# Four-layer dense graph network on one core: first transfers in another order, narrower idle products, one chunk pair's features turned by VectorE, and a block of last-row work started later

## The chip, the cores and the metric

The kernel runs on one core of one Trainium2 chip. The metric is the time of one execution on the device in microseconds (us); the time shown before the change is the median of three runs. The profile is one further execution, recorded by the hardware profiler.

## The reference, cut to what matters

There are N = 3327 nodes with D = 64 features each, `x`, and one symmetric weighted adjacency matrix `adj` (3327 x 3327, about half a per cent of it other than zero). Four layers follow each other, each with a layer norm and a relu ahead and a residual behind. Every layer multiplies by the adjacency matrix or by a function of it, eight times in all.

```
def ggc(x, adj, W, wih, whh, bih, bhh):              # layer 0 has two of these cells
    gi = (adj @ (x @ W)) @ wih.T + bih
    gh = x @ whh.T + bhh
    r, z = sigmoid(gi_r + gh_r), sigmoid(gi_z + gh_z)
    n = tanh(gi_n + r * gh_n)
    return (1 - z) * n + z * x

h = relu(layernorm(x)); x = x + relu(ggc(relu(ggc(h, adj, ...1)), adj, ...2))   # k = 0, 1
h = relu(layernorm(x)); x = x + w(adj) @ (h @ weight) + bias                    # k = 2
#   w: mask of adj, each row's last 100 non-zeros weighted 0.5 ** (distance from the last)
h = relu(layernorm(x)); x = x + three times ((adj * adj) @ x) @ W.T + b         # k = 3, 4, 5
h = relu(layernorm(x)); x = x + two times tanh([adj @ x, x] @ W)                # k = 6, 7
```

## The kernel before, in words

**Tiles.** The nodes are padded to 3328 = 26 blocks of 128, kept as two halves `s` of 13 blocks. The 13 columns of blocks are cut into four chunks `c` of 3, 3, 3 and 4 blocks (`CH`); chunks 0 and 1 are group 0, chunks 2 and 3 are group 1. Features are kept in two forms: node-major tiles `y[k][c]` (128 nodes on the partitions, then block, half, feature), which are the stationary operands of the big products, and feature-major tiles `both[c]` (64 features of either half on the partitions, nodes along the row), on which the gates of a cell work.

**The big products.** For each of the eight steps `k`, each source block `q` and each chunk `c`, line 614 multiplies the 128 x 64 features of the block with the block's row of the transposed adjacency (384 or 512 columns for each of the two halves) into a PSUM bank `sum`. The row of a source block for one group is one tile `adj`, 768 KB for group 0 and 896 KB for group 1, read from memory by one DMA of SyncE's queue (line 412) into one of 20 slots. A tile is used for two steps where the order of sources allows it: `alone(0, 0)` runs step 0 of group 0, `joint(1, 0)` steps 0 and 1 of group 1, `joint(0, 1)` steps 1 and 2 of group 0, and so on, up to `alone(0, 7)`. Within `joint(1, 0)` step 1 takes its sources in the order: chunks 0 and 1, then chunk 2 (its half 0, then its half 1), then chunk 3 (the same).

**The order of the work.** Each engine works through its own instruction stream in order. The streams are written by one recorder, `run()`, which goes through the list of big products; after each of them it lets `spend` count down small tasks that were begun earlier and records their next part when their number of us has run out. These numbers are `yield`s: they are written by hand and decide where in the streams a piece of work stands, not when it runs. Slots, half slots for masks (`Mask`) and PSUM banks are handed out in the order of recording, and waits follow from reads and writes.

**The start.** SyncE's queue issues, in this order, the first three blocks of `x`, tile 0 of `adj`, the next blocks of `x` (`load_x(*CH[1])`), tiles 1 and 2, the last seven blocks of `x`, tile 3, the weights and the bias columns of the first cell (`load_cell`, lines 154 and 157), and from there on the tiles as slots come free. `warm_up` (line 177) issues 14 products of 384 columns whose result nobody reads. VectorE meanwhile makes the layer norm of chunk 0 and begins that of chunk 1 (lines 841 to 856; the power -0.5 on line 852 is GpSimd's).

**The counts.** Beside step 0, VectorE writes each tile as a 0/1 mask (line 473) into a half slot and TensorE sums it over source blocks (line 549), some tiles behind the product of the same tile.

**The cell.** When a chunk's sums of step 0 or 1 are complete, `gru` runs: `evacuate_stacked` copies half 0 of the sums to `both` on ScalarE (line 831) and half 1 on VectorE (line 832), TensorE makes three or four gate products from `both` (line 883), ScalarE the sigmoids (888) and the tanh (904), VectorE the rest (893 to 912), and ScalarE writes one of the two relus (915). After the first cell `after_0` turns the features back into the node-major form: `stacked_to_nodes` multiplies pieces of 64 nodes with an identity (line 781, 4 products of 64 columns for each block) and VectorE copies the result from PSUM (line 951). `transpose_on_vector` (line 810) and `sums_to_nodes` (line 826), used in later layers, turn features the other way, in squares of 32 by 32 on VectorE.

**The last rows.** The masks of step 2 give up row 127 to a row of counts, so that the 26 sources in row 127 are handled by themselves: `last_sources(g)` clears a half slot on GpSimd (line 571), loads the rows by two DMAs of SyncE's queue (575), makes one mask operation (577) and one combination with the counts (581) on VectorE and a conversion on ScalarE (583), over 768 or 896 columns. Its result is read at the end of step 2 of its group. It is begun with `later_task(130.0, ...)` for group 0 and `later_task(155.0, ...)` for group 1. In step 2 the products with `tri` (line 314) are evacuated to `e` alternately by ScalarE (530) and VectorE (528), three products ahead of their use on line 614.

Of the kernel before, what the change touches and what calls it, by code (L numbers as in the profile page):

```python
# [44 lines left out]
N, D = 3327, 64  # L45
P = 128
NB = 13
# [4 lines left out]
CH = [(0, 3), (3, 6), (6, 9), (9, 13), (3, 5), (5, 6)]  # L52
NC = 4
PARTS = (4, 5)
CWM = 512
GROUPS = [(0, 1), (2, 3)]
# [8 lines left out]
W1, IH1, HH1, W2, IH2, HH2 = 0, 1, 4, 7, 8, 11  # L65
# [26 lines left out]
def upper(n):  # L92
    return slice(n * D, (n + 1) * D)
# [3 lines left out]
def kernel(  # L97
# [9 lines left out]
    nc = tc.nc  # L107
# [7 lines left out]


    xs = const.tile([P, NB, 2, D], F32, name="xs")
    def load_x(g0, g1):
        nc.sync.dma_start(out=xs[:, g0:g1], in_=x[:, g0:g1])

    load_x(*CH[0])
    slots = [const.tile([P, 2, GWM], F32, name=f"adj{i}") for i in range(NBUF)]
    mhalf = const.tile([P, 8], F32, name="mhalf")
    nc.gpsimd.memset(mhalf, -0.5)
# [3 lines left out]
    stage = const.tile([P, 7 * D + NBIAS], F32, name="stage")  # L128
    w3 = const.tile([P, 2, 2, D], F32, name="w3")
    both = [const.tile([P, 2, (b1 - b0) * P], F32, name=f"both{c}") for c, (b0, b1) in enumerate(CH[:NC])]  # L130
# [4 lines left out]
    ident = const.tile([P, P], F32, name="ident")  # L135
# [15 lines left out]
                            compare_op=ALU.is_gt, fill=0.0, base=2 - P, channel_multiplier=1)  # L151

    def load_cell(cell):
        nc.sync.dma_start(out=stage[upper(0), :7 * D].rearrange("p (w f) -> p w f", f=D),
                          in_=weights[:, (W1, W2)[cell]:(W1, W2)[cell] + 7])
        if cell == 0:
            nc.sync.dma_start(out=stage[upper(0), 7 * D:], in_=bias_cols)

    def unfold_cell(cell):

# [11 lines left out]
    def warm_up():  # L172

        i, ps = take()
        for n in range(7):
            for h in range(2):
                nc.tensor.matmul(ps[upper(h), :width(0)], xs[:, 0, h, :], flat(xchunk(0)), start=True, stop=True)
        give(i)

    def fold_cell(cell):  # L180
# [67 lines left out]
    def more_constants():  # L248
# [32 lines left out]
        for c in range(NC):  # L281
            yield 4.0
            ahead_of_cell(c)
        yield 47.0
        load_cell(1)
        yield 20.0
        unfold_cell(1)
# [15 lines left out]
    def blocks(c):  # L303
        return CH[c][1] - CH[c][0]

    def width(c):
        return blocks(c) * P
# [15 lines left out]
    def take(sums=False, either=True):  # L323


        either = either and not sums
        pool = idle_sums if sums else idle_temps
        if either and idle_sums and (not pool or released[idle_sums[0]] < released[pool[0]]):
            pool = idle_sums
        for c in list(tasks):  # L330
            if not pool and c not in running:
                advance(c)
        i = pool.popleft()
        return i, banks[i]

    def give(i):
        released[i] = max(released) + 1
        (idle_sums if i < 4 else idle_temps).append(i)

    def nodes(c):  # L340

        return feat.tile([P, blocks(c), 2, D], F32, name=f"y{c}")

    def flat(t):
        return t.rearrange("p b s d -> p b (s d)")
# [4 lines left out]
    def xchunk(c):  # L350
        return xs[:, CH[c][0]:CH[c][1]]

    def view(ps, c):
        return ps[:, :width(c)].rearrange("p (b f) -> p b f", f=P)
# [5 lines left out]
    def advance(c):  # L360
        running.add(c)
        try:
            tasks[c][1] = next(tasks[c][0])
        except StopIteration:
            del tasks[c]
        running.discard(c)

    def begin(c, task):
        finish(c)
        tasks[c] = [task, 0.0]  # L370
        advance(c)

    def finish(c):
        while c in tasks:
            advance(c)

    def later_task(us, task):
        yield us
        yield from task
# [185 lines left out]
    def last_sources(g):  # L565

        w = sum(width(c) for c in GROUPS[g])
        w0 = CH[GROUPS[g][0]][0] * P
        room = Mask(w)
        v = room.view.rearrange("p s w -> p (s w)").bitcast(F32)  # L570
        nc.gpsimd.memset(v, 0.0)  # L571
        yield 4.0
        rows = adjT.rearrange("(q p) (s n) -> q p s n", p=P, s=2)
        for s in range(2):
            nc.sync.dma_start(out=v[s * D:s * D + NQ], in_=rows[:, P - 1, s, w0:w0 + w])
        yield 12.0
        nc.vector.tensor_scalar(v, v, 0.0, 129.0 * TWO7, op0=ALU.not_equal, op1=ALU.mult)
        for c in GROUPS[g]:
            finish(("count", c))
        yield 1.0  # L580
        nc.vector.scalar_tensor_tensor(v, totals[g], -TWO7, v, op0=ALU.mult, op1=ALU.add)
        yield 1.5
        nc.scalar.activation(lastw[g], v, AF.Relu, bias=bitsb)
        room.free()
# [37 lines left out]
    units = []  # L622
# [151 lines left out]
    def stacked_to_nodes(c, w):  # L774

        i, ps = take()
        v = view(ps, c)
        for b in range(blocks(c)):
            for s in range(2):
                for n in range(2):  # L780
                    nc.tensor.matmul(v[upper(n), b, upper(s)], both[c][:, s, b * P + n * D:b * P + (n + 1) * D], w(s),  # L781
                                     start=True, stop=True)
        return i, v
# [43 lines left out]
                yield 1.2  # L827
        return yk

    def evacuate_stacked(acc, c):  # L830
        nc.scalar.copy(both[c][upper(0), 0], acc[0][1][upper(0), :width(c)])  # L831
        nc.vector.tensor_copy(both[c][upper(1), 1], acc[1][1][upper(1), :width(c)])  # L832
        for i in {acc[0][0], acc[1][0]}:
            give(i)

# [36 lines left out]
    def gru(acc, c, bi, bh, cell, pace=1.0):  # L872

        w = width(c)
        evacuate_stacked(acc, c)
        yield 0.8 * pace
        at = dead.popleft()
        r, z, d = (slots[at].rearrange("p s w -> p (s w)")[:, i * CWM:i * CWM + w] for i in range(3))

        def gate(g):  # L880
            i, ps = take()
            for s in range(2):
                nc.tensor.matmul(ps[upper(1 - s), :w], cells[:, cell, s, g, :], both[c][:, s], start=True, stop=True)
            return i, ps

        for g, v in enumerate((r, z)):
            i, ps = gate(g)
            nc.scalar.activation(v, ps[:, :w], AF.Sigmoid, bias=bsum[:, cell, g:g + 1])
            give(i)
        nh = None if cell == 0 else gate(2)  # L890
        ni = gate(3)
        yield 1.0 * pace
        nc.vector.scalar_tensor_tensor(r, ahead[c] if nh is None else nh[1][:, :w], bcol[:, bh + 2:bh + 3], r,
                                       op0=ALU.add, op1=ALU.mult)
        nc.vector.tensor_tensor(r, r, ni[1][:, :w], ALU.add)
        give(ni[0])
        if nh is not None:
            give(nh[0])
        else:
            del ahead[c]  # L900
            if not any(ch in ahead for ch in GROUPS[c // 2]):
                rooms[c // 2].free()
        yield 1.0 * pace
        nc.scalar.activation(r, r, AF.Tanh, bias=bcol[:, bi + 2:bi + 3])
        yield 0.8 * pace
        for s in range(2):
            u = upper(1 - s)
            nc.vector.tensor_tensor(d[u], both[c][u, s], r[u], ALU.subtract)
        nc.vector.tensor_tensor(d, d, z, ALU.mult)
        nc.vector.tensor_tensor(d, d, r, ALU.add)  # L910
        if cell == 0:
            nc.vector.tensor_scalar(both[c][upper(0), 1], d[upper(0)], 0.0, None, op0=ALU.max)
        yield 2.4 * pace
        if cell == 0:
            nc.scalar.activation(both[c][upper(1), 0], d[upper(1)], AF.Relu)
            yield 1.0 * pace
        return at, d
# [27 lines left out]
    def after_0(c, acc):  # L945
        at, _ = yield from gru(acc, c, BI1, BH1, 0)
        dead.append(at)
        i, v = stacked_to_nodes(c, lambda s: ident[:, upper(1 - s)])
        yield 0.8
        yk = nodes(c)  # L950
        nc.vector.tensor_copy(flat(yk), v)
        give(i)
        y[1][c] = yk

    def after_1(c, acc):
# [62 lines left out]
    def after_7(c, acc):  # L1018
# [9 lines left out]
        nc.scalar.dma_start(out=out[:, g0:g1], in_=xs[:, g0:g1])  # L1028

    after[:] = [after_0, after_1, after_2, after_3, after_4, after_5, after_6, after_7]  # L1030


# [8 lines left out]
    alone(0, 7, sweep=6, parts=True)  # L1041

    nc.gpsimd.memset(stage, 0.0)
    first = list(dict.fromkeys(t for _, _, t in units))[:4]
    first[0].load()
    load_x(*CH[1])
    first[1].load()
    first[2].load()
    load_x(CH[2][0], NB)
    first[3].load()  # L1050
    load_cell(0)
    warm_up()
    for c in (0, 0, 0, 1, 0, 1, 1):
        if c in tasks:
# [4 lines left out]
    begin(2, later_task(4.0, before_0(2)))  # L1059
    begin(3, later_task(10.0, before_0(3)))  # L1060
    begin(NC + 1, later_task(130.0, last_sources(0)))
    begin(NC + 2, later_task(155.0, last_sources(1)))
    run()
    for c in list(tasks):
        finish(c)
# [39 lines left out]
```

## Time and profile before

| What | Value |
|---|---|
| median of 3 runs | 703.85 us (703.73 to 704.52) |
| the profiled execution | 704.14 us, of which the span of the program's own instructions is 702.2 us |
| TensorE, matrix products | 684.9 us busy, 98% of the span |
| VectorE | 348.8 us, 50% |
| ScalarE | 271.9 us, 39% |
| GpSimd | 80.5 us, 11% |
| bytes moved | 201.31 MB, 287 GB/s in the mean, 400 to 406 GB/s in each 10 us between 20 and 100 us |

The page gives the busy time of each engine over the span and in 40 slices of 17.6 us, the traffic, and the costliest groups of instructions, each with the idle time of its engine just before it and what ended most of that idle time. A matrix product of 32-bit numbers appears as two records, and its weight load is recorded apart (PEld). Records of products overlap, since the products are pipelined; the distance from one start to the next tells the pace. A busy share is a mean over stages that have different limits, so the stages are read one by one below.

### The profile page before, as it was taken

What the parts mean: (1) busy time and instruction counts of PE and PEld (TensorE: products, weight loads), DVE (VectorE), ACT (ScalarE), POOL (GpSimd) and SP (SyncE); (2) the same over time, 40 slices, a digit from 0 to 9 for tenths busy, and PEclk for the clock granted to TensorE, in tenths of its full rate; (3) what the DMA queues carried; (4) which work ended last, traced back from release to release, by engine and by line L of the source; (5) the groups of instructions that cost most, each with busy time, mean ns of one, the idle gap of its engine ahead of it and who ended that gap; (6) DMA issues with size and microseconds to landing.
All of it is one profiled execution on the core that took longest, in us unless ns stands there. A gap on an engine that the chain in (4) does not pass through costs nothing.

```text
span 702.2 us, 12670 instructions
## 1 busy us (share of the span) xinstructions
PE 684.9 (98%) x5128; PEld 378.0 (54%) x5128; DVE 348.8 (50%) x746; ACT 271.9 (39%) x422; POOL 80.5 (11%) x114
## 2 busy tenths in 40 slices
PE   7998999999999999999999999999999999999997
PEld 3684667744566686446444444333444444344586
DVE  4945835733997889747533106425271565005101
ACT  1112100212146878888998206832166600000101
POOL 5300000002284233011100000000000000000000
PEclk9999999999999999999999999999999999999999
DMA  8999998089776943683799659963998399917991
GB/s 312 401 402 404 406 406 278 1 295 401 252 240 257 385 162 101 235 290 100 268 386 347 237 179 408 405 250 122 385 366 270 107 398 405 406 73 273 403 403 49
DMA packets 68693, 201.31 MB, mean 287 GB/s; under 512 B 7244, under 2 KB 8372, under 8 KB 68636
## 3 DMA queue, kind: packets, MB, share of 16 engines
q1 hardware_dynamic: 65740, 199.46, 76.3%
q8 instruction: 40, 0.66, 0.4%
q10 hardware_dynamic: 720, 0.85, 0.3%
q0 software_dynamic: 2176, 0.20, 0.2%
q14 instruction: 17, 0.14, 0.1%
HBM read 199.45 MB, written 0.85 MB: 285 GB/s over the span
## 4 chain that ended last, share of the span: by engine, by line
PE 58%; DVE 1%; ACT 0%; POOL 0%; issue 0%; ACTq 0%; DVEq 0%; POOLq 0%
PE sum L614 54%; PE temp L314 3%; PE temp L781 1%; POOL st L852 0%; DVE xs L1026 0%; ACT t L1023 0%; DVE both L832 0%; ACT both L831 0%; DVE e L528 0%; ACTq L1028 0%; PE sum L314 0%; DVE y L848 0%; DVE t L843 0%; DVE y L856 0%; DVE st L849 0%
## 5 line engine op out<-in xcount | busy, mean ns | idle before, releaser
L614 PE MATMUL sum<-adj,y 128*64 128x384 f32 (+3 forms) x3016 | 535.8, 501 | 3.7 <-DMA adj<-in_adjT 2.5
L614 PEld LDWEIGHTS sum<-adj,y 128*64 128x64 f32 x3016 | 247.0, 137 | 233.8 <-issue 193.9
L447 ACT ACTIVATE adj<-adj 128x768 f32<-128x768 f32 (+1 forms) x176 | 144.2, 891 | 45.2 <-PE sum L614 22.8
L473 DVE TENSOR_SCALAR adj<-adj 128x768 bf16<-128x768 f32 (+3 forms) x208 | 113.5, 597 | 32.6 <-PE temp L549 24.7
L614 PE MATMUL sum<-e,both 128*64 128x384 bf16 (+1 forms) x624 | 73.9, 339 | 0.5 <-DVE e L528 0.5
L530 ACT ACTIVATE e<-temp,bitsb 128x384 int16<-128x384 f32 (+1 forms) x120 | 67.5, 608 | 14.4 <-PE temp L314 8.1
L831 ACT COPY both<-sum 64x384 f32<-64x384 f32 (+3 forms) x17 | 8.1, 478 | 151.2 <-PE sum L614 150.1
L832 DVE COPY both<-sum 64x384 f32<-64x384 f32 (+3 forms) x17 | 9.6, 568 | 109.7 <-ACT both L831 109.7
L852 POOL TENSOR_TENSOR st<-st,mhalf 128x6 f32<-128x6 f32 (+1 forms) x16 | 24.8, 1553 | 288.3 <-DVE st L850 288.3
L449 DVE TENSOR_TENSOR adj<-adj 128x768 f32<-128x768 f32 (+1 forms) x32 | 30.6, 1005 | 52.0 <-DMA adj<-in_adjT 33.3
L314 PE MATMUL temp<-adj,tri 128*64 128x384 bf16 (+1 forms) x332 | 51.4, 341 | 1.3 <-DVE e L528 1.2
L614 PEld LDWEIGHTS <-both 128*64 128x64 bf16 x624 | 41.2, 110 | 19.0 <-issue 6.5
L528 DVE TENSOR_SCALAR e<-temp 128x384 int16<-128x384 f32 (+1 forms) x46 | 28.3, 617 | 20.8 <-ACT e L530 10.9
L314 PEld LDWEIGHTS <-tri 128*64 128x64 bf16 x416 | 28.9, 110 | 17.4 <-issue 9.0
L478 POOL DMA_DIRECT2D adj<-totals x52 | 31.5, 607 | 51.6 <-PE temp L314 44.6
L810 DVE STREAM_TRANSPOSE both<-y 32x96 f32<-32x96 f32 (+1 forms) x128 | 35.6, 278 | 2.9
L549 PE MATMUL temp<-adj,behind 128*64 128x384 bf16 x208 | 33.7, 340 | 2.8 <-DVE adj L473 2.8
L826 DVE STREAM_TRANSPOSE y<-t 32x96 f32<-32x96 f32 (+1 forms) x64 | 17.8, 278 | 25.4 <-ACT t L817 24.5
L549 PEld LDWEIGHTS <-behind 128*64 128x64 bf16 x208 | 20.3, 110 | 16.6 <-issue 13.0
L762 DVE COPY t<-sum 128x384 f32<-128x384 f32 x6 | 3.3, 555 | 34.9 <-PE sum L614 34.9
L187 ACT COPY t<-temp 128x128 f32<-128x128 f32 x1 | 0.3, 266 | 48.2 <-PE temp L185 48.2
L571 POOL MEMSET adj<- 128x768 f32 (+1 forms) x2 | 1.9, 950 | 137.6 <-PE sum L614 137.6
(130 smaller groups left out, 353.3 us busy)
## 6 DMA issues: line engine op xcount, KB each, us to landing
adj<-in_adjT SPq DMA_DIRECT2D x130, 768.0 KB, 8.9
adj<-in_adjT SPq DMA_DIRECT2D x104, 896.0 KB, 12.1
xs<-in_x SPq DMA_DIRECT2D x1, 448.0 KB
adj<-totals POOLq DMA_DIRECT2D x26, 3.0 KB, 5.0
adj<-totals POOLq DMA_DIRECT2D x26, 3.5 KB, 3.2
xs<-in_x SPq DMA_DIRECT2D x2, 192.0 KB, 2.5
out<-xs ACTq DMA_DIRECT2D x2, 192.0 KB
out<-xs ACTq DMA_DIRECT2D x1, 256.0 KB
```

What stands on the lines that cost most here:

```text
L314: nc.tensor.matmul(out[hs], lhsT[:, hs], rhs, start=start, stop=stop)
L447: nc.scalar.activation(sq, v, AF.Square)
L449: nc.vector.tensor_tensor(sq, v, v, ALU.mult)
L473: nc.vector.tensor_scalar(t.mask.view[:rows, half], t.view()[:rows, half], 0.0, None, op0=ALU.not_equal)
L478: nc.gpsimd.dma_start(out=t.mask.view[P - 1:P], in_=totals[t.g][t.q:t.q + D + 1:D, :])
L528: nc.vector.tensor_scalar(wide[:, s], ps[:, :w], BITS, 0.0, op0=ALU.add, op1=ALU.max)
L530: nc.scalar.activation(wide[:, s], ps[:, :w], AF.Relu, bias=bitsb)
L549: nc.tensor.matmul(counts[c][1][s * D:(s + 1) * D, :w], behind[:, NQ - 1 - t.q:NQ - 1 - t.q + D], t.mask.view[:, s, t.cols(c)], start=firs ...
L614: nc.tensor.matmul(acc[h][1][h * D:(h + 1) * D, :w], yq[h], rhs[h], start=first and n == 0, stop=last and n == len(terms) - 1)
L810: nc.vector.transpose(to[at:at + 32, :, q], h[q * 32:(q + 1) * 32, :, s, f * 32:(f + 1) * 32])
L826: nc.vector.transpose(yk[q * 32:(q + 1) * 32, :, s, f * 32:(f + 1) * 32], v[at:at + 32, :, q])
L852: nc.gpsimd.tensor_tensor(st[:, 3, :n], st[:, 2, :n], mhalf[:, :n], ALU.pow)
```

## The change

The first blocks of `x` and the weights and bias columns of the first cell are issued from ScalarE's queue, except for the first three blocks of `x`, which stay on SyncE's; tile 0 of `adj` follows there at once. The idle products have 192 columns in place of 384. In the first cell `evacuate_stacked` makes both of its copies on ScalarE. `after_0` turns the features of chunks 2 and 3 by VectorE: for each half, eight operations of 32 partitions by 3 or 4 blocks of 32, in place of the products of line 781 and the copy of line 951. `last_sources(1)` is begun with 200 in place of 155; in the instruction streams its two VectorE operations then stand among the last operations of the stretch in which the second half of the layer norms of step 2, group 0, is made, its two DMAs stand 12 tile loads later in SyncE's queue, its memset behind four of the DMAs of the masks' last rows in GpSimd's, and its conversion behind the second tile of squares in ScalarE's. No other instruction of the four compute engines changes its place; some take another PSUM bank or slot.

```diff
--- before.py
+++ after.py
@@ -115,10 +115,8 @@
 
 
     xs = const.tile([P, NB, 2, D], F32, name="xs")
-    def load_x(g0, g1):
-        nc.sync.dma_start(out=xs[:, g0:g1], in_=x[:, g0:g1])
-
-    load_x(*CH[0])
+    for queue, (g0, g1) in ((nc.sync, CH[0]), (nc.scalar, CH[1]), (nc.scalar, (CH[2][0], NB))):
+        queue.dma_start(out=xs[:, g0:g1], in_=x[:, g0:g1])
     slots = [const.tile([P, 2, GWM], F32, name=f"adj{i}") for i in range(NBUF)]
     mhalf = const.tile([P, 8], F32, name="mhalf")
     nc.gpsimd.memset(mhalf, -0.5)
@@ -151,10 +149,11 @@
                             compare_op=ALU.is_gt, fill=0.0, base=2 - P, channel_multiplier=1)
 
     def load_cell(cell):
-        nc.sync.dma_start(out=stage[upper(0), :7 * D].rearrange("p (w f) -> p w f", f=D),
-                          in_=weights[:, (W1, W2)[cell]:(W1, W2)[cell] + 7])
+        queue = nc.sync if cell else nc.scalar
+        queue.dma_start(out=stage[upper(0), :7 * D].rearrange("p (w f) -> p w f", f=D),
+                        in_=weights[:, (W1, W2)[cell]:(W1, W2)[cell] + 7])
         if cell == 0:
-            nc.sync.dma_start(out=stage[upper(0), 7 * D:], in_=bias_cols)
+            queue.dma_start(out=stage[upper(0), 7 * D:], in_=bias_cols)
 
     def unfold_cell(cell):
 
@@ -174,7 +173,7 @@
         i, ps = take()
         for n in range(7):
             for h in range(2):
-                nc.tensor.matmul(ps[upper(h), :width(0)], xs[:, 0, h, :], flat(xchunk(0)), start=True, stop=True)
+                nc.tensor.matmul(ps[upper(h), :3 * D], xs[:, 0, h, :], xs[:, 0:3, 0], start=True, stop=True)
         give(i)
 
     def fold_cell(cell):
@@ -827,9 +826,12 @@
                 yield 1.2
         return yk
 
-    def evacuate_stacked(acc, c):
+    def evacuate_stacked(acc, c, on_scalar=False):
         nc.scalar.copy(both[c][upper(0), 0], acc[0][1][upper(0), :width(c)])
-        nc.vector.tensor_copy(both[c][upper(1), 1], acc[1][1][upper(1), :width(c)])
+        if on_scalar:
+            nc.scalar.copy(both[c][upper(1), 1], acc[1][1][upper(1), :width(c)])
+        else:
+            nc.vector.tensor_copy(both[c][upper(1), 1], acc[1][1][upper(1), :width(c)])
         for i in {acc[0][0], acc[1][0]}:
             give(i)
 
@@ -872,7 +874,7 @@
     def gru(acc, c, bi, bh, cell, pace=1.0):
 
         w = width(c)
-        evacuate_stacked(acc, c)
+        evacuate_stacked(acc, c, on_scalar=cell == 0)
         yield 0.8 * pace
         at = dead.popleft()
         r, z, d = (slots[at].rearrange("p s w -> p (s w)")[:, i * CWM:i * CWM + w] for i in range(3))
@@ -945,11 +947,20 @@
     def after_0(c, acc):
         at, _ = yield from gru(acc, c, BI1, BH1, 0)
         dead.append(at)
-        i, v = stacked_to_nodes(c, lambda s: ident[:, upper(1 - s)])
-        yield 0.8
         yk = nodes(c)
-        nc.vector.tensor_copy(flat(yk), v)
-        give(i)
+        if c in GROUPS[0]:
+            i, v = stacked_to_nodes(c, lambda s: ident[:, upper(1 - s)])
+            yield 0.8
+            nc.vector.tensor_copy(flat(yk), v)
+            give(i)
+        else:
+            for s in range(2):
+                v = both[c][upper(1 - s), s].rearrange("p (b q n) -> p b q n", q=4, n=32)
+                for f in range(2):
+                    for q in range(4):
+                        nc.vector.transpose(yk[q * 32:(q + 1) * 32, :, s, f * 32:(f + 1) * 32],
+                                            v[f * 32:(f + 1) * 32, :, q])
+                    yield 0.6
         y[1][c] = yk
 
     def after_1(c, acc):
@@ -1041,13 +1052,6 @@
     alone(0, 7, sweep=6, parts=True)
 
     nc.gpsimd.memset(stage, 0.0)
-    first = list(dict.fromkeys(t for _, _, t in units))[:4]
-    first[0].load()
-    load_x(*CH[1])
-    first[1].load()
-    first[2].load()
-    load_x(CH[2][0], NB)
-    first[3].load()
     load_cell(0)
     warm_up()
     for c in (0, 0, 0, 1, 0, 1, 1):
@@ -1059,7 +1063,7 @@
     begin(2, later_task(4.0, before_0(2)))
     begin(3, later_task(10.0, before_0(3)))
     begin(NC + 1, later_task(130.0, last_sources(0)))
-    begin(NC + 2, later_task(155.0, last_sources(1)))
+    begin(NC + 2, later_task(200.0, last_sources(1)))
     run()
     for c in list(tasks):
         finish(c)
```

## The prediction

> **What bounds the kernel now.** I read the busy shares, then who TensorE waited for up to 80 us, then TensorE's and VectorE's timelines around those waits.
>
> ```profile
> PE 684.9 (98%) x5128; PEld 378.0 (54%) x5128; DVE 348.8 (50%) x746; ACT 271.9 (39%) x422; POOL 80.5 (11%) x114
> ```
>
> ```profile
> PEld sum L614 <- DMA adj<-in_adjT: 6.3, 12, 2.3
> ```
>
> TensorE is the bound over the whole, so every product taken away is worth its time unless a wait takes its place; the second line (the waits over the span) says that weight loads still waited for tiles. Where these waits lie decides about the start:
>
> ```profile
> 54.89 1.51 PE L614 MATMUL sum<-adj,y 128*64 128x384 f32 x8 [0.19 <-DMA adj<-in_adjT]
> ...
> 60.77 0.87 PE L614 MATMUL sum<-adj,y 128*64 128x384 f32 x4 [0.75 <-DMA adj<-in_adjT]
> ...
> 67.36 0.32 PE L549 MATMUL temp<-adj,behind 128*64 128x384 bf16 x1 [0.95 <-DVE adj L473]
> ```
>
> TensorE catches up with the transfers at 54.89 us and takes the last tiles of group 0 at intervals of about 1.95 us (54.89, 56.84, 58.83, 60.77), the time of 768 KB at 401 GB/s. Up to 60.77 us the tiles set the end, and what TensorE saves before is waited away there. After 60.77 us no transfer stops it. At 67.36 us it waits for a mask instead. VectorE's timeline says why:
>
> ```profile
> 62.19 0.56 DVE L832 COPY both<-sum 64x384 f32<-64x384 f32 x1 [3.74 <-ACT both L831]
> ...
> 66.16 0.56 DVE L832 COPY both<-sum 64x384 f32<-64x384 f32 x1 [1.88 <-ACT both L831]
> 66.75 0.56 DVE L473 TENSOR_SCALAR adj<-adj 128x768 bf16<-128x768 f32 x1
> ```
>
> VectorE stood 3.74 and 1.88 us in front of a copy of finished sums, with masks queued behind it. Two more places concern the change, the turning of chunks 2 and 3 (timeline of TensorE, then VectorE) and the last-row work of group 1 (VectorE, then TensorE):
>
> ```profile
> 143.44 1.11 PE L781 MATMUL sum<-ident,both 128*64 128x64 f32 x22
> ...
> 149.83 1.10 PE L781 MATMUL temp<-ident,both 128*64 128x64 f32 x32
> ```
>
> ```profile
> 144.66 0.56 DVE L951 COPY y<-sum 128x384 f32<-128x384 f32 x1 [3.03 <-PE sum L781]
> ...
> 225.78 0.62 DVE L577 TENSOR_SCALAR adj<-adj 128x896 f32<-128x896 f32 x1
> ...
> 230.95 1.08 DVE L581 SCALAR_TENSOR_TENSOR adj<-totals,adj 128x896 f32<-128x896 bf16 x1
> ```
>
> ```profile
> 233.81 0.82 PE L314 MATMUL temp<-adj,tri 128*64 128x384 bf16 x4 [0.91 <-DVE e L528]
> ...
> 280.62 0.65 PE L614 MATMUL sum<-e,both 128*64 128x384 bf16 x5 [0.46 <-DVE e L528]
> ```
>
> In both stretches of the last two lines TensorE waits for VectorE: 24.36 of 26 us busy from 220 to 246, 22.59 of 24 from 262 to 286, while VectorE has 22.80 and 23.15.
>
> **What the skill says.** The Trainium skill, "DMA: Bandwidth & Descriptors", section Issuing engines are not separate DMA queues: transfers of all issuers share the same 16 engines, and a second issuer saves only the time of issuing. The trace agrees in that SyncE spends 0.4 to 0.7 us on each issue and the engines are full from 4 us on (402 GB/s), so no bandwidth is to be won later. "TensorE: Matmul & The Clock Gate", Part 1: the array starts at half clock, needs about 3.4 us of activity, and falls back after an idle window of that length. The trace fits: idle products start 0.64 us per pair until 6.57 us, then 0.32. "VectorE: DVE Perf Modes", section The three transpose paths: VectorE turns squares of 32 by 32 only, from SBUF to SBUF; line 826 shows such operations of 32x96 0.28 us apart and line 810 those of 32x128 0.30 to 0.32 apart.
>
> **The change part by part.**
>
> *First transfers.* The engines moved 186 GB/s between 2 and 3 us and 138 between 3 and 4 (windows of the trace), 402 in the next: (216 + 264) GB/s times 1 us, 0.48 MB or 1.2 us of traffic, were lost while SyncE's issues followed each other. ScalarE is free until 12.93 us and can issue 0.64 MB of `x` from 0.8 us on. I take two thirds, **-0.8 us**, for every later tile, and so for TensorE at 60.77. Bounds: 0, if the two issuers hinder each other, to -1.7, if also the dip between 13 and 16 us (330 GB/s, 0.54 us), where weights and biases are moved, goes. ScalarE's queue: two issues, then the weights wait for GpSimd's memset of `stage` (over at 2.39 us), and behind them stands only the table load, needed at 12.93: free. SyncE's loads are behind nothing new. Sharing the engines, the first `x` may land up to 0.5 us after its 3.34 us; this lies before the binding tile and costs nothing.
>
> *Layer norm and idle products.* VectorE's line 841 of chunk 1 waited 1.47 us for `x` (to 7.54) and held line 856 of chunk 0 (8.81) behind it; with `x` early, 856 can follow GpSimd's power (over at 7.50), and TensorE can start near 8.2 in place of 9.47. The idle products, half as wide, end near 7.3 (3.2 us at half clock, then 2 pairs of 0.16 us) and not at 9.3. All this is worth **0**: the cover is the wait for tiles up to 60.77 us. If the clock fell back in the gap, some 1.6 us at 8 us would meet about 2.0 us of pace lost before the four late tiles; without that cover it would be paid.
>
> *Copies on ScalarE, chunks 0 and 1.* VectorE no longer stands at 832, so the mask of 66.75 us can be made as soon as TensorE's earlier counts free its half slot, near 65.4. Line 883 of chunk 1 started at 67.37 behind that count; now it waits for the second ScalarE copy instead: sums done 65.60, two copies of 0.47 behind each other, 66.6, of which the first half of a product hides a part. That gives **-0.8 us** (0 if the half slot comes late, -1.2 if the wait goes whole). Behind the added copy on ScalarE stand the table load and the sigmoid, 0.25 us later than 63.70, with VectorE's 893 at 67.22 as their reader: free. The next waits at 74.61 and 79.47 (0.5 and 0.4 us) are at the end of chains that move along, and stay. For chunks 2 and 3 there was no wait at TensorE to remove: 0.
>
> *Turning, chunks 2 and 3.* TensorE loses 12 and 16 products of 64 columns: 143.38 to 144.38, 0.99 us with the gap in front, and 0.95 us; together -1.94. In their place VectorE gets 16 operations of 0.284 and 16 of 0.315, less two copies of 0.56 and 0.69. In the built streams the first eight stand ahead of the rest of chunk 3's gates (908 to 912), the others behind it. They start when ScalarE's relu is written (142.2): half 0 of chunk 2 at 144.45; TensorE, having 5 products of line 614 from 140.38 (3 x 0.86 + 2 x 0.64), wants it at 144.24: stall 0.2. Then 1.39 + 0.69 + 0.69 + 0.42 of gates with small hops to 147.7, eight more squares to 150.0; TensorE wants half 1 three tiles of 1.5 us after 144.45, at 148.95: stall 1.0. Chunk 3: half 0 at 152.5, wanted at 154.5; half 1 at 155.0, wanted at 157: hidden. Net -1.94 + 1.2 = **-0.7 us**; bounds -1.9 (no stall) and +0.3 (each operation and hop a quarter slower).
>
> *Last-row work.* Taken from 225.78 and 230.95: 0.62 + 1.08 us of VectorE and 1.04 us of ScalarE (at 232.06, after 1.25 us of idleness waiting for it). The first fills partly a wait for the tanh, so VectorE is 0.3 + 1.0 us earlier and TensorE's waits at 231.08 and 233.81 shrink: **-1.3 us** (0 to -2.0). Put back near 281 us, between masks and evacuations of a VectorE that is idle for 0.4 us in 20, ahead of the evacuations that ran at 281.03 and 283.23: the first 0.6, the second 1.7 us late, in front of TensorE's waits of 281 to 284: **+1.5 us** (0 to +1.7, and +1.0 more if the conversion holds back ScalarE, which had 1.28 us idle there). The two DMAs move past 12 loads on SyncE and wait there for GpSimd's memset; the loads behind are for tiles whose masks are made over 30 us later (load near 245, mask near 283): free. GpSimd's memset (1.16 us) falls between two of its DMAs at 249.91 and 259.34: free. If a slot came so late that these covers were gone, TensorE would wait for a tile's mask, us for us.
>
> **Sum.** -0.8 - 0.8 - 0.7 - 1.3 + 1.5 = -2.1 us. Against the profiled execution's 704.14 us (span 702.2) that is 702.0; it lay 0.29 above the median of the runs, so **701.7 us**. A difference of 0.2%, 1.4 us, is about what a measurement can tell from none.
>
> **Rivals.** (A) The sum holds: 700.3 to 702.4, chance 0.53. (B) *The early gains don't arrive*: the issuers share what fills the engines, the tile at 60.77 comes as late as before, and the half slot keeps the mask at its place. Left: -0.7 - 1.3 + 1.5, 703.3 us, no difference. For it: the engines are full from 4 us on; against it: 0.48 MB of empty engine time. 0.25. (C) *VectorE near 281 us is the bound*: what is put there is paid in full, 1.7 us and 1.0 of the conversion, and ScalarE idles again for the combination (1.25 as at 232), while nothing returns at 225 because ScalarE, 20.42 of 26 us busy there, was as late. Price 4.0 against gains of 2.3: 705.5 us; it decides once the price is over 2.3. For it: 23.15 of 24 us; against it: ScalarE's idle 1.28 us and VectorE's slack after 285.8. 0.14. (D) *Everything at its good end*, the moved block hidden by products of step 3, which need no evacuation: -1.7 - 1.0 - 1.0 - 1.3, 698.9 us, 0.08.
>
> **The numbers.** The range runs from between (D) and (A), 699.7, to between (B) and (C), 704.6, leaving out most of (D) and (C). Faster 0.60 (A nearly whole, and D), same 0.26 (B and A's edge), slower 0.14 (C).
>
> **What would show it.** Right: 2 to 4 us of the windows near 300 GB/s and more; the tile of 60.77 near 60.0; no line 832 for the first cell and a wait before line 883 of chunk 1 of a few tenths; no line 781 at 143 and 150, and two waits for VectorE's transposes, 0.2 and 1.0 us; shorter waits near 231 to 234, longer ones near 281 to 284. The forecast is wrong if TensorE waits more than 2 us in all for the transposes, if the tile of 60.77 has not moved, or if the stretch from 262 to 286 grows by over 2 us.

## The result, and the profile after

The changed kernel takes **699.64 us** (median of 4 runs, 699.51 to 700.19) against 703.82 us of the kernel before on the same chip (4 runs): a ratio of 0.9940, 95% interval 0.9923 to 0.9957. That is 4.2 us, twice the forecast 2.1. The profiled execution has a span of 697.6 us (702.2 before).

The first line of the page's busy shares for the kernel after, which answers to the one shown of before:

```profile
PE 680.2 (97%) x5072; PEld 377.9 (54%) x5072; DVE 354.5 (51%) x772; ACT 274.4 (39%) x426; POOL 79.1 (11%) x114
```

TensorE has 56 records fewer (28 turning products, two records each) and 4.7 us less to do, of which narrower idle products are a part; VectorE has 26 instructions and 5.7 us more.

The waits of TensorE in the kernel after (who waited for whom, us in total, times, longest):

```profile
PE temp L548 <- DVE adj L472: 2.5, 4, 1.3
PE sum L613 <- DVE e L527: 2.3, 3, 1.2
...
PE sum L613 <- DVE y L961: 0.7, 1, 0.7
...
PE sum L613 <- DMA adj<-in_adjT: 0.4, 1, 0.4
```

There is one wait for the transposes and, for tiles, 0.4 us of the products and 2.4 us of the weight loads (5 waits, where 12 with 6.3 us were shown before); the wait for `e` is the one that the moved last-row work was expected to lengthen. The same in the timeline of TensorE (start, duration, idle time before):

```profile
58.07 0.87 PE L613 MATMUL sum<-adj,y 128*64 128x384 f32 x4
...
63.38 2.33 PE L885 MATMUL sum<-both,cells 128*64 128x384 f32 x11
...
65.92 3.49 PE L613 MATMUL sum<-adj,y 128*64 128x384 f32 x17
...
146.17 1.29 PE L613 MATMUL sum<-adj,y 128*64 128x384 f32 x6 [0.72 <-DVE y L961]
...
276.14 0.81 PE L613 MATMUL sum<-e,both 128*64 128x512 bf16 x5 [0.61 <-DVE e L527]
...
279.21 1.08 PE L613 MATMUL sum<-adj,y 128*64 128x512 f32 x4 [1.19 <-DVE e L527]
```

The last of these products in the timeline of before, for comparison:

```profile
283.83 1.08 PE L614 MATMUL sum<-adj,y 128*64 128x512 f32 x4 [0.19 <-DVE e L528]
```

The first line is the product that started at 60.77 us before, now 2.70 us earlier. The product shows no wait for its tile, but its weight load waited 0.47 us for it, and the tile landed at 58.03 us, so the transfers still set this start. Gates and products from 63 to 69 us follow each other without the wait for a mask that stood at 67.36. At 146.17 is the stall that VectorE's squares cause; at 276 and 279 is the price of the moved work. The two waits of 0.29 and 0.91 us at 231 and 234 us before are gone.

Setting the start of each big product (line 613 after, 614 before) against the same product before gives the account of these two profiles: -2.70 us at the last tile of group 0, -3.78 by 143 us, -4.57 behind the stall at 146, -4.83 by 205, -6.17 by 235, -4.62 by 286, -4.61 at the end. (The 0.3 us gained near 177 us were not followed up.) Read alone, this says that the first transfers brought 2.7 us, over three times the forecast. The experiments show that this reading is wrong.

### The profile page after: what moved, and what is told of

Same layout as the page of the kernel before. It is cut to its first block, busy times and chain, and to the rows that moved or that the text cites. A ratio compares the mean times of both kernels' runs of the same rounds, so it can differ in the third digit from the quotient of the medians.

```text
span 697.6 us, 12581 instructions
## 1 busy us (share of the span) xinstructions
PE 680.2 (97%) x5072; PEld 377.9 (54%) x5072; DVE 354.5 (51%) x772; ACT 274.4 (39%) x426; POOL 79.1 (11%) x114
## 4 chain that ended last, share of the span: by engine, by line
PE 86%; DVE 8%; DMA 3%; POOL 2%; issue 1%; ACT 1%; ACTq 0%; DVEq 0%; POOLq 0%
PE sum L613 73%; PE temp L313 5%; DMA adj<-in_adjT 2%; PE temp L548 2%; PE temp L885 2%; DVE adj L472 2%; PE sum L313 1%; PE sum L885 1%; PE temp L780 1%; DVE e L527 1%; DVE adj L910 1%; POOL both L251 1%; DVE y L961 1%; POOL st L854 1%; DVE st L851 1%
## 5 line engine op out<-in xcount | busy, mean ns | idle before, releaser
L834 DVE COPY both<-sum 64x384 f32<-64x384 f32 (+3 forms) x13 | 7.2, 560 | 98.6 <-ACT both L830 98.6
L477 POOL DMA_DIRECT2D adj<-totals x52 | 34.8, 671 | 46.3 <-PE temp L313 32.4
```

The lines of the kernel that those rows point to most:

```text
L477: nc.gpsimd.dma_start(out=t.mask.view[P - 1:P], in_=totals[t.g][t.q:t.q + D + 1:D, :])
```

## The experiments

Differences below are of medians, each kernel against the kernel before on the same chip (704.25, 703.98, 704.07 and 703.94 us in the four groups); in brackets the ratio with its 95% interval. Where a kernel is set against the changed kernel, that is its 699.64 us from the first measurement; before itself lay between 703.82 and 704.25 us in the groups, so a few tenths can't be told this way. "Shift" means the start of a big product against the same product in the profile of before, or of after where so said.

**1. The load changes alone, whole and in parts.** `transfers`: all of the new order and the second queue, on the kernel before. `x_on_scalar`: only the later parts of `x`. `x_ahead_on_sync`: all of `x` ahead of tile 0, everything on SyncE. `w_on_scalar`: only weights and biases.

```diff
 transfers        = x_on_scalar + w_on_scalar
 x_on_scalar:     -    load_x(*CH[1]) ... load_x(CH[2][0], NB)       # SyncE, between tiles
                  +    nc.scalar.dma_start(...CH[1]); nc.scalar.dma_start(...CH[2][0]:NB)
 x_ahead_on_sync: +    nc.sync.dma_start(...) for all three parts, ahead of tile 0
 w_on_scalar:     -    nc.sync.dma_start(out=stage...)
                  +    nc.scalar.dma_start(out=stage...)             # cell 0 only
```

> Only the first transfers are changed (x from the second chunk on, weights and bias columns from ScalarE's queue). The product that waited last for a tile of group 0 stood at 60.77 us before and at 58.07 after the whole change. Theory 'lost traffic' (the prediction's): 1.2 us of traffic filled in the first 4 us, so that product near 59.6 and the kernel 1.2 us faster. Theory 'out of step': besides, the 16 engines no longer run out of step, the slowest one gains, product near 58.1, kernel 2.7 us faster. Theory 'product pace': the tile is early only because the other edits make TensorE faster; product above 60.

> Only the second and third part of x go to ScalarE's queue; weights and bias columns stay on SyncE's behind tile 3. If the start of the transfers (2 to 4 us) holds the gain: product of 60.77 near 58.1 to 58.6, kernel 2.2 to 2.7 us faster. If the small weight and bias rows in the middle of SyncE's queue (the dip at 13 to 16 us) hold most of it: product near 59.6, kernel 1.2 us faster.

> All of x stands ahead of tile 0 on SyncE's own queue; nothing is issued by ScalarE. If order alone matters: as with x on ScalarE's queue, product of 60.77 near 58.1 to 58.6. If the second issuer matters (issues of 0.4 to 0.7 us beside each other): part of the lost traffic stays, product near 59.5 to 60.5, kernel up to 1.2 us faster.

> Only the weights and bias columns of the first cell go to ScalarE's queue. If the dip at 13 to 16 us costs what its traffic says: product of 60.77 near 60.2, kernel 0.5 us faster. If the small rows throw the engines out of step: product near 59.3, kernel 1.5 us faster. If they don't matter: no change.

Measured: `transfers` 702.99 us, -1.26 (0.9984, 0.9976 to 0.9991); `x_on_scalar` 702.68, -1.57 (0.9983, 0.9974 to 0.9992); `x_ahead_on_sync` 704.39, +0.14 (1.0001, 0.9992 to 1.001); `w_on_scalar` 703.39, -0.86 (0.9991, 0.9982 to 0.9999). The second queue counts; `x` ahead on one queue doesn't. With all of `x` ahead on SyncE the DMA engines still move only 200 GB/s between 3 and 4 us, with `x` on ScalarE 399, with both parts 410 (138 before). The dip between 13 and 16 us, 330 GB/s before, is there with `x` alone on ScalarE (337) and gone with the weights there (399, both parts 401). Over the first 20 us the engines moved 323 GB/s before, 322 with `x` ahead on SyncE, 328 with the weights on ScalarE, 341 with `x`, and 346 with both: in traffic the parts add. In time they don't seem to (-1.57 and -0.86 against -1.26), but each interval is about 0.6 us to either side.

Two things did not fit. The shift at the last tile was -2.51 us in `transfers`, twice its gain at the end: 1.09 to 1.26 us were lost again near 211 us, in all four kernels, in front of the gates. The timeline of TensorE in `transfers` shows it:

```profile
211.22 1.18 PE L882 MATMUL temp<-both,cells 128*64 128x384 f32 x5 [0.63 <-DVE both L831]
```

And `x_ahead_on_sync`, worth nothing, had a shift of -1.11 there too.

**2. The other three parts alone, and the last-row work put back.**

```diff
 copies:   +  scalar.copy for half 1 in evacuate_stacked (cell 0)
 turn:     +  after_0 with VectorE's squares for chunks 2 and 3
 late:     -  later_task(155.0, last_sources(1))
           +  later_task(200.0, last_sources(1))
 after155: the changed kernel with 155.0 again
```

> Before, with only the first cell's second copy of finished sums moved from VectorE to ScalarE. If the copy was what held the mask up, the count's wait at 67.4 us (1.20 us in all) goes and TensorE is 1.2 us early from 69 us on; the pair with the transfers would then be additive up to 100 us. Theory 'TensorE, once early, meets GpSimd's memset among VectorE's 13 masks at 205 us': about 1.0 of it is lost again at 211 us, end -0.2. Rival 'that loss belongs to the early transfers': no gap at 211 us, end -1.2.

> Before, with only chunks 2 and 3 of the first cell turned by VectorE. TensorE loses 28 small products, 1.94 us, and waits once for the transposes at 146 us, 0.9: -1.0 us from 178 us on, as in the whole change. Theory of the memset at 205 us: the gap of 1.0 us at 211 us comes here too, end 0. Rival: no gap, end -1.0.

> Before, with only group 1's last-row work begun at 200 instead of 155. -1.3 us at 231 to 234, +1.5 at 281 to 284: +0.2 us at the end, if its worth doesn't depend on the rest. Rival (it also keeps the memset out of VectorE's masks): alone it shows nothing of this, since before has no gap at 211 us; so again +0.2, and the difference appears only in the next kernel.

> The changed kernel with group 1's last-row work begun at 155 again. If its place is worth the same everywhere: the waits of 231 to 234 come back (+1.3), those of 276 to 280 go (-1.5): 0.2 us faster than the changed kernel, 699.4. Theory of the memset at 205 us: it falls among the 13 masks again because TensorE is early, +1.0 at 211 us: 0.8 slower than the changed kernel, 700.4.

Measured: `copies` 702.67, -1.31 (0.9983, 0.9974 to 0.9991); `turn` 703.35, -0.63 (0.9993, 0.9987 to 1.0); `late` 703.01, **-0.97** (0.9987, 0.998 to 0.9994), where +0.2 was expected; `after155` 700.55, +0.91 over the changed kernel. In `after155` the waits came and went as forecast (+1.32 by 232 us, -1.56 at 277 to 282, shifts against the kernel after), and 1.26 us more were lost between 206 and 214. So the move of the last-row work is worth 0.9 to 1.0 us, alone as in the whole, and its forecast had missed a term. In `late`, whose memset stands at 256.54 us, nothing is lost near 211 us.

The profiles of `copies`, `turn` and `late` gave a second surprise. None of them touches the first transfers, yet the product of 60.77 us started at 59.08, 59.06 and 59.56.

**3. The kernel before, profiled again.** No edit.

> The kernel before, unchanged, profiled once more. Four profiles share its first transfers (before, and the kernels with only the copies, the turning or the late start changed), yet their last tile product of group 0 started at 60.77, 59.08, 59.06 and 59.56 us. Theory 'the start differs from execution to execution, and the profile of before had a late one': the product lies between 59 and 61 us here, and where it is early (under 60) the memset falls among VectorE's 13 masks and 1.0 to 1.3 us are lost again near 212 us. Rival 'those edits made the start earlier': 60.7 us again, no gap near 212 us.

> The kernel before once more, for the same two theories: a start between 59 and 61 us with the loss near 212 us where it is early, or 60.7 us and no loss.

Measured: 704.12 and 705.05 us, with the product at 59.59 and 60.16 us. The timeline of TensorE in `again1`:

```profile
59.59 0.87 PE L614 MATMUL sum<-adj,y 128*64 128x384 f32 x4 [0.74 <-DMA adj<-in_adjT]
...
213.03 1.18 PE L883 MATMUL temp<-both,cells 128*64 128x384 f32 x5 [0.81 <-DVE both L832]
```

The shift against the profile of before is -1.17 us up to 210 us and +0.10 from 216 on: the early start is there, and is lost at 213.03. VectorE and GpSimd of `again1` show how (timelines):

```profile
204.76 7.62 DVE L473 TENSOR_SCALAR adj<-adj 127x768 bf16<-127x768 f32 x13
212.41 0.56 DVE L832 COPY both<-sum 64x384 f32<-64x384 f32 x1
```

```profile
205.14 2.23 POOL L935 DMA_DIRECT2D lasty<-both  x4 [1.73 <-DVE both L928]
207.36 0.86 POOL L571 MEMSET adj<- 128x896 f32 x1
```

Thirteen masks take 7.62 us; twelve take 0.54 to 0.59 us and the fifth, begun at 206.68 and running while the memset of `last_sources(1)` runs, takes 1.96. The copy of the sums stands behind them, and TensorE's gates wait for the copy. In `late`, with the same four DMAs but without the memset behind them, the thirteen take

```profile
204.71 6.26 DVE L473 TENSOR_SCALAR adj<-adj 127x768 bf16<-127x768 f32 x13
```

In the profile of before the same stretch, again VectorE and then GpSimd:

```profile
205.75 6.19 DVE L473 TENSOR_SCALAR adj<-adj 127x768 bf16<-127x768 f32 x13
```

```profile
206.13 7.43 POOL L935 DMA_DIRECT2D lasty<-both  x4 [0.74 <-DVE both L928]
213.56 1.16 POOL L571 MEMSET adj<- 128x896 f32 x1
```

Here it is GpSimd that was held up: the first of its four DMAs took 5.90 us, until the masks were over, and the memset came behind the copy; there it met another mask (1.28 us at 213.85), which held nothing of TensorE's up. The Trainium skill, "SBUF — State Buffer", section Who interferes with whom, says that VectorE in a two-port mode and GpSimd contend for one pair of ports, and that the one that issues first has it for its whole instruction while the other is blocked. The traces agree in that either engine can be the one that stands; that the masks run in such a mode, no run here shows. By the recorded starts they don't agree on who has the ports: in all nine profiles with a loss the mask began 0.67 or 0.68 us ahead of the memset and was still the one that was held. The mask lost 1.4 us, more than the 0.86 us that the memset is recorded with; recorded spans on GpSimd are rough.

In ten of the profiles the memset of group 1 stands at this place of GpSimd's stream. Nine have one mask of 1.95 or 1.96 us and lose 1.09 to 1.27 us near 211 us; only the profile of before, which had the latest start of all, does not. Why its late start let VectorE through is not settled.

**4. The memset itself.** `memset_on_scalar` is `after155` with the memset made by ScalarE.

```diff
-        nc.gpsimd.memset(v, 0.0)
+        nc.scalar.activation(v, xs[:, 0:7]..., AF.Copy, scale=0.0)   # group 1
```

> The changed kernel with group 1's last-row work at 155 again, but its memset made by ScalarE (a copy with scale 0) and not by GpSimd. If the memset beside VectorE's masks is what costs the 0.92 us at 209.55, VectorE's 13 masks take 6.2 to 6.3 us and not 7.62, the gap goes or shrinks to a few tenths, and it is about 0.9 faster than the kernel with 155: 699.6 us, with the waits of 231 to 234 still there. Rival 'something else at 155 holds the masks, such as GpSimd's DMAs': 7.6 us again, 700.5 us.

Measured: 700.22 us, 0.33 faster than `after155` and not 0.9. The mechanism is as expected, the timeline of VectorE has

```profile
201.03 6.25 DVE L472 TENSOR_SCALAR adj<-adj 127x768 bf16<-127x768 f32 x13
```

and the gap of 0.59 us that `after155` has at 209.55 is gone. But the clearing takes ScalarE 0.95 us at 199.13, directly ahead of two conversions to `e`, and TensorE pays there:

```profile
200.60 0.32 PE L616 MATMUL sum<-e,both 128*64 128x384 bf16 x1 [0.34 <-ACT e L529]
```

The shift against the kernel after is +0.01 before, +0.89 at 205 us. So the memset beside the masks is the cause, shown by taking it away; made by ScalarE on this stretch it cost 0.88 us, nearly what was won.

**5. Two parts taken out of the changed kernel.** `wide_idle`: idle products of 384 columns again. `no_turn`: TensorE turns chunks 2 and 3 again.

> The changed kernel with the idle products at 384 columns again. The prediction put their shortening at 0, with the waits for late tiles as its cover. These waits are gone in the changed kernel: the first product comes 1.4 us later, and what of it is left at 58 us is the question. Theory 'tiles still set the pace until TensorE has caught up': 0.2 us slower (699.85). Rival 'the cover is gone': 1.0 to 1.4 slower (701).

> The changed kernel with chunks 2 and 3 of the first cell turned by TensorE again. With a steady start and no memset at 205 us, the worth of the turning shows unmixed: 1.0 us slower, 700.65. Rival 'worth what it showed alone, 0.63 by the medians': 700.3.

Measured: `wide_idle` 700.11 us (699.45 to 700.55), its profile +0.17 at the end; the first product is 1.91 us later, of which 0.25 is left at 60 us, no more than the scatter of that start from profile to profile (57.96 to 58.53 us): TensorE waits less for tiles and masks on the way. `no_turn` 700.27 us, +0.63: the same as the turning brought alone (whose interval reaches zero). Its shift against the kernel after at 146 us is 0.78 more than at 60: 1.69 us of products without the 0.91 us of stall (the stall by product starts, as the kernel `best` below sheds it; the timeline shows 0.72 of it as idle).

**6. Better places.** `after105` and `after120` begin group 1's last-row work at 105 and 120 in the changed kernel. `best` has 105, and turns both halves of chunk 2 before chunk 3's gates:

```diff
-    begin(NC + 2, later_task(200.0, last_sources(1)))
+    begin(NC + 2, later_task(105.0, last_sources(1)))
...
-                    yield 0.6
+                    if s or c != GROUPS[1][0]:
+                        yield 0.6
```

> The changed kernel with group 1's last-row work begun at 105 in place of 200: its VectorE operations then stand near 155 us, where VectorE idles, and its memset far from the masks at 205 us. The waits of 276 to 280 us go (-1.5), those of 231 to 234 stay away, no gap at 210 us: 1.5 faster than the changed kernel, 698.1 us. Rival 'what is put there delays the turning or the last rows of group 0': less than 0.5 gained.

> The same begun at 120: VectorE operations near 165 us. The same gain, 698.1 us, if any idle place of VectorE serves; rival as for 105.

> The changed kernel with group 1's last-row work begun at 105 and both halves of chunk 2 turned ahead of chunk 3's gates (16 squares in a row, then lines 910 to 914). The wait of 0.91 us at 146 goes, since half 1 is written near 142.6 and wanted at 145.5; chunk 3 is ready 2.25 us later, before it is wanted: 0.9 faster than the kernel with 105 alone, 697.4 us. Rival 'chunk 3 becomes late': a wait of 1 us or more for its transposes, 698.3 or more.

Measured: `after105` 698.28 us, 1.36 faster than the changed kernel (0.9914 of before, 0.9901 to 0.9928); `after120` 699.86, no gain; `best` **697.15** (0.9906, 0.9892 to 0.992), 2.5 us faster than the changed kernel and 6.8 faster than before. In `after120` group 1's work did not stand near 165 us, where VectorE has room, but from 181 to 185, where VectorE was busy for 3.90 of 4 us in the kernel after; everything behind it slid, the same work of group 0 too, whose conversion came onto ScalarE at 198.99 (197.02 in the kernel after), ahead of the conversions that TensorE needs; TensorE's timeline:

```profile
201.68 0.32 PE L613 MATMUL sum<-e,both 128*64 128x384 bf16 x1 [1.00 <-ACT e L529]
```

So this run did not test an idle place; it shows what a full one costs. In `best` the squares, the gates behind them, the squares of chunk 3 and the last-row work follow each other on VectorE:

```profile
138.26 4.54 DVE L961 STREAM_TRANSPOSE y<-both 32x96 f32<-32x96 f32 x16 [0.57 <-ACT both L917]
...
146.44 5.07 DVE L961 STREAM_TRANSPOSE y<-both 32x128 f32<-32x128 f32 x16 [0.32 <-ACT both L917]
151.54 0.63 DVE L576 TENSOR_SCALAR adj<-adj 128x896 f32<-128x896 f32 x1
152.20 1.09 DVE L580 SCALAR_TENSOR_TENSOR adj<-totals,adj 128x896 f32<-128x896 bf16 x1
```

and TensorE has no wait from 136.66 to 156.53 us:

```profile
136.66 20.07 PE L613 MATMUL sum<-adj,y 128*64 128x512 f32 x108
```

## Why the forecast was wrong, step by step

| Step | forecast | alone | in the whole |
|---|---|---|---|
| first transfers, idle products | -0.8, 0 | -1.26 (without the narrower idle products) | -1.46 (mean start of nine profiles against mean of six) |
| copies on ScalarE | -0.8 | -1.31 | -1.08 (shift, 60 to 143 us) |
| turning | -0.7 | -0.63 | -0.63 (taken out; shift -0.79) |
| last-row work | +0.2 | -0.97 | -0.91 (put back) |
| sum | -2.1 | -4.17 | -4.1; measured -4.2 |

The direction was right and the size was not: 699.64 lies just outside the range given, at its fast end. Of the 2.1 us missing, by the column "alone", about 1.2 are the last-row work, 0.5 the copies and 0.5 the transfers. The intervals of single parts are 0.5 to 0.6 us to either side, so the division between the last two is rough; the sign of the first is not.

**Last-row work: the step that failed.** Its two terms were right: -1.3 forecast and -1.33 measured at 231 to 234 us, +1.5 and +1.55 at 276 to 279. But the step looked only at where the memset goes ("falls between two of its DMAs at 249.91 and 259.34: free") and put what it leaves at nothing, without a reason. It leaves a place where it holds VectorE's masks up and costs TensorE 1.1 to 1.3 us, in nine of ten profiles. The profile of before did not show this, because in this one execution the memset came after the copy; its one sign of trouble was the DMA of 5.90 us beside the masks.

**Why a profile with a typical total misled.** Six profiles with the old first transfers have the last tile's product at 60.77, 60.16, 59.59, 59.56, 59.08 and 59.06 us: mean 59.70. The profile of before was 1.07 us late at this product and lacked a loss of about 1.27 us later (the size in `again1`). The two cancel, so that its 704.14 us lay near the median, and nothing in its total gave a warning. The lateness didn't come from the first transfers: the seventh tile from the end of group 0 landed at 47.41 us, against a mean of 47.56 in the six, and the fourth from the end at 54.84, 7.43 us later, where the other five have 5.84 to 5.87. So 1.57 us were lost in between, in full traffic (403 GB/s from 50 to 60 us); `again1` lost 0.64 us one tile later. What held these tiles up is not known. The nine profiles with the new transfers have a mean start of 58.24 us: 1.46 less than 59.70, within the bounds of 0 to 1.7 that the prediction gave, and not the 2.70 of the direct comparison.

**First transfers.** Here the mis-sized term is the dip. Two thirds of the 1.2 us of lost traffic, 0.8 us, was about right: over the first 4 us the engines moved 156 GB/s in place of 88, which is 0.27 MB or 0.7 us at 401 GB/s (138 to 411 GB/s between 3 and 4 us). But the prediction read that "no bandwidth is to be won later" and left the dip between 13 and 16 us to the far end of its bounds. It went as well (330 to 401 GB/s), which is another 0.5 us; together that is what `transfers` gained. Rival (B), that the issuers share what fills the engines, is refuted by 399 to 411 GB/s with a second issuer against 200 with one and all of `x` ahead. The cover given for the idle products held: at most 0.25 us of 1.91 came through.

**Copies.** The direction and the place were right and the size was not. The wait at 67.36 us went whole, since the half slot was free in time, and brought 1.0 us of shift by 70 us; the few tenths forecast in front of the gates did not come: the second ScalarE copy was hidden. About 0.1 us was lost again by 100 us, and 0.2 more was gained near 140 us, at the gates of chunk 3, where the prediction had put 0.

**Turning.** Right, by errors that cancel: 1.69 us of products where 1.94 were counted, one stall of 0.91 where 0.2 and 1.0 were. The second stall was forecast to within 0.1 us of place and size; the first did not appear.

**Rivals.** (C) needed the block near 277 us to cost more than 2.3 us; it cost 1.55, and ScalarE's conversion held nothing back. (D), 698.9 us, was nearest in number but not in kind: its hidden block did not happen.

## What to carry to other kernels

One profile is one draw. Where a stretch hangs on transfers, profile the same kernel again before pricing anything that follows it: two repeats here moved the landing by 0.6 and 1.2 us and uncovered a loss that the first did not have. When work is moved, price what it leaves as well as where it goes, GpSimd's memsets and DMAs beside VectorE among it. And look in the trace where a moved block really came to stand: begun at 105 it stood where VectorE idled and was worth 1.4 us (`after105`), begun at 120 it stood in a full stretch, pushed what follows back, on ScalarE too, and was worth nothing (`after120`).

## What was not expected of the hardware

- A GpSimd memset of 128x896 (0.86 us) lengthened a VectorE mask that ran with it from 0.55 to 1.96 us; with the same work in another phase, a DMA issue of GpSimd took 5.90 us behind VectorE's masks.
- With the old first transfers, all on one queue, the product of the last tile of group 0 started between 59.06 and 60.77 us in six executions. In the nine kernels with `x` and weights both on the second queue it lies between 57.96 and 58.53. The transfers set it there too: where the landing of that tile is recorded, in six of the nine, it is 0.04 to 0.17 us ahead of the product. Part of the old spread is the 1.57 and 0.64 us that two profiles of the kernel before lost between 47 and 56 us; none of the nine shows such a loss. Whether the new order prevents it, or nine executions did not happen to have it, is not shown.
